# Block sums kept in SBUF for the quarter sums, filter loads moved into the last attention, two convolution steps in halves

## The chip, the cores and the metric

The kernel runs on one core of one Trainium2 chip. The metric is the device time of one execution in microseconds (us). In what follows PE is the matrix engine, DVE the vector engine, ACT the scalar engine, POOL the engine that also issues one set of DMAs, and SP the engine that issues the others. Line numbers (L236) are those of the kernel before.

## The reference, cut to what matters

Two layers run one after the other on x of shape (4, 1024, 32, 32). The first is an attention block with rotary angles and RMS norms over all channels, the second a bottleneck of three convolutions with batch norms.

```python
# layer 0, for 4 batches of N = 1024 tokens, 16 heads of 64
qkv = (x @ w_qkv.T + b_qkv).reshape(B, N, 3, nh, hd)
q, k = rope(q), rope(k)
q = rmsnorm(q.reshape(B, N, inner), q_norm_w);  k = rmsnorm(k.reshape(B, N, inner), k_norm_w)
attn = softmax(einsum('bqhd,bkhd->bhqk', q, k) * hd ** -0.5)
ctx  = einsum('bhqk,bkhd->bqhd', attn, v).reshape(B, N, inner)
x    = rmsnorm(ctx @ w_proj.T, norm_out_w) + x
# layer 1
out = relu(bn(conv1x1(x, w1)));  out = relu(bn(conv3x3(out, w2)));  out = bn(conv1x1(out, w3))
x   = relu(x + softplus(residual_scale)[0] * out)
```

## The kernel before, in words

**Stages.** The batches b = 0 to 3 go one after the other through Q projection, K projection, V projection, attention (two halves c of 512 queries, eight head pairs hp each) and output projection. Then come the first convolution, the 3x3 convolution (written as transforms of input, filter and output around 16 products) and the third convolution. All operands are float32.

**Fast matrix products.** Each projection is a 2x2 block product in seven instead of eight block products. For this the weights need four sums of blocks, S1 to S4, made by four subtractions or additions on DVE. Q and K of batch 0 use one level: `project` (L290 and on) runs, for each of four column groups g, five products of eight matmul records each (S2, S1, S3, S4, A22), after eight products on unsummed blocks. Its sums are made by `operands` (L236 to L239: the third subtraction, L238, makes the operand of the group's first product), from four blocks that SP loads (L226), into a ring of eight chunks `wring`; POOL stores the four sums to DRAM (`wd`, L242). V of batch 0 and everything after it use two levels (`project2`): each of the seven block operands (index k in `OUTER`) is cut into quarters and needs sums of quarters, which lie in DRAM as `wd2`.

**The weight work of batch 0.** What V of batch 0 reads from `wd` and `wd2` is made beside Q and K of batch 0. `prepare_blocks` loads the four blocks of v's weights for one g on POOL's queue (L406), and its `make` forms the four sums on DVE (L409 to L412) and stores them to `wd` (L414). `prepare` does the same one level down: four quarter loads on POOL's queue (L383), four subtractions or additions (L392 to L395), four stores to `wd2` (L397). For k of S1 to S4 the quarters are read back from `wd`. `weight_parts(parts, first, step, lag, alloc)` sets the order: part i is loaded after `first + i * step` products and made `lag` products later. In Q of batch 0 the parts are the four blocks of v and v's quarters k = 0, 1, 6, 2, in the tile `unused`; in K of batch 0 v's quarters 3, 4, 5 and then q's quarters k = 0 for the next batches, in the tile `room` (traced as `rq`), which V writes afterwards.

**Order.** PE and POOL, and in the main region DVE and ACT too, execute in the order in which the program emits the steps: `after(n, step)` emits a step n products later, `waiting` holds the steps of the rotary turn (`turn(f)`, L701 for q: two products with sin and cos on DVE and two accumulating DMAs on POOL, L705) that fill DVE's spare time. `turn` writes into one of three `big_temp` buffers, so it waits until the DMAs of the turn three before have read theirs. SP's order is left to a scheduler. POOL's DMAs take eight completion semaphores in turn, so that each waits for the one eight before it.

**Filters.** `filters()` loads nine pieces of the 3x3 filter on SP (L1053) into the tiles T0 to T2 (traced as `t_w`), and returns five steps that transform them; the attention of the last batch spreads the steps over its head pairs as `extra`. In SP's built order the nine loads stand among those of v's weights of the last batch, three at a time.

**Rotary tables.** The tables cos and sin are multiplied by the row norm in place (L693) and so are loaded again on POOL's queue after every use (L176, L177).

**Convolutions.** `across(i, j)` and `down(b, i, row, j)` are the two steps of the input transform, both through `differences` (L1325); `first_channels` runs them for batch 0 and the first 128 channels, between the last matmuls of the first convolution. After the 3x3 convolution, when the statistics are complete, the norm and Relu of h2 run tile by tile, batches 0 and 2 on ACT (L1428) and 1 and 3 on DVE (L1430, L1431), ahead of the third convolution (L1526), whose first group takes the batches in order.

Of the kernel before, what the change touches and what calls it, by code (L numbers as in the profile page):

```python
# [12 lines left out]
AF = mybir.ActivationFunctionType  # L13
ALU = mybir.AluOpType
# [7 lines left out]
NT = C // P  # L22
# [7 lines left out]
NPT = PL // P  # L30
# [4 lines left out]
WQ, WK, WV, WP, W1 = 0, NFB, 2 * NFB, 3 * NFB, 4 * NFB  # L35
# [27 lines left out]
NG = NT // 2  # L63
QH = P // 4
SUMS = ("S2", "S1", "S3", "S4")
OUTER = ("A11", "A12", "S2", "S3", "S1", "S4", "A22")
TARGET = ("22", "11", "12", "21", "22", "12", "21")
QT = CH // 2
# [17 lines left out]
def program(ctx, tc, x, wblk, w2, w3, vecs, cos, sin, out, bad):  # L86


    nc = tc.nc
# [62 lines left out]
    wd2 = dram.tile([4, len(OUTER), len(SUMS), P, CH], F32, name=f"wd2{u}")  # L152
# [5 lines left out]
    with tc.tile_pool(name=f"st{u}", bufs=2) as st, ExitStack() as s:  # L158
# [26 lines left out]
        half = [slice(c * CH, (c + 1) * CH) for c in range(NCH)]  # L185
# [68 lines left out]
        def after(n, step):  # L254
            later.append((pace["at"] + n, step))
# [145 lines left out]
        def prepare_blocks(base, g, alloc, queue):  # L401

            a11, a12, a21, a22 = a = alloc(f"blk_{base}_{g}")
            for i, t in enumerate(a):
                ih = i % 2
                queue.dma_start(t, wblk[base + g + NG * (i // 2)][:, ih * NH * P : (ih + 1) * NH * P])  # L406

            def make():
                nc.vector.tensor_tensor(a22, a21, a22, ALU.add)  # L409
                nc.vector.tensor_tensor(a21, a11, a21, ALU.subtract)  # L410
                nc.vector.tensor_tensor(a11, a22, a11, ALU.subtract)
                nc.vector.tensor_tensor(a12, a12, a11, ALU.subtract)  # L412
                for o, t in enumerate((a11, a22, a21, a12)):
                    nc.gpsimd.dma_start(wd[base // NT * NG + g, o], t)  # L414

            return make

# [628 lines left out]
        def filters():  # L1046

            steps = []
            raw = t_tiles("w2")
            taps = w2.rearrange("p (c k f) -> p c k f", c=NPT, k=9)  # L1050
            for dy in range(3):
                for dx, slot in enumerate((0, 1, 3)):
                    nc.sync.dma_start(  # L1053
                        raw[dy][:, slot, :].rearrange("p (c f) -> p c f", c=NPT), taps[:, :, 3 * dy + dx, :]
                    )
            two = [tp.tile([P, 2, CH], F32, tag=n, name=f"u2_{n}") for n in ("cos", "sin")]

            def sums_of(g0, g1, g2, new):

                nc.vector.tensor_tensor(new, g0, g2, ALU.add)  # L1060
                nc.scalar.mul(g1, g1, 0.5)
                nc.vector.scalar_tensor_tensor(g1, new, 0.5, g1, ALU.mult, ALU.add)
                nc.vector.tensor_tensor(new, new, g1, ALU.subtract)

            for dy in range(3):
                r = raw[dy]
                steps.append(lambda r=r: sums_of(r[:, 0], r[:, 1], r[:, 3], r[:, 2]))
            for h in range(2):
                js = slice(2 * h, 2 * h + 2)
                steps.append(lambda h=h, js=js: sums_of(*(raw[dy][:, js] for dy in range(3)), two[h]))  # L1070
            for i in range(4):
                for j in range(4):
                    uw[i, j] = two[j // 2][:, j % 2] if i == 2 else raw[(0, 1, None, 2)[i]][:, j]
            return steps
# [19 lines left out]
        def weight_parts(parts, first, step, lag, alloc):  # L1094

            for i, part in enumerate(parts):
                after(first + i * step, lambda part=part: after(lag, part(alloc, nc.gpsimd)))

        def pieces_of(tile, cols=NCH):

            at = deque(tile[:, i, h] for i in range(tile.shape[1]) for h in half[:cols])

            def alloc(name):
                at.rotate(-4)
                return [at[i] for i in range(-4, 0)]

            return alloc


        parts_of = {  # L1110
            base: [
                lambda alloc, queue, which=which, base=base, k=k: prepare(which, base, k, alloc, queue)
                for k in range(len(OUTER))
            ]
            for which, base in enumerate((WQ, WV, WP, WK))
        }

        def blocks_of(base):
            return [lambda alloc, queue, g=g: prepare_blocks(base, g, alloc, queue) for g in range(NG)]
# [15 lines left out]
        room = v_room("rq_0")  # L1135
        for b in range(B):
# [7 lines left out]
            two = (0, *two2[0], False) if b > 0 else None  # L1144
            if b == 0:
                unused = kp.tile([P, NT, N], F32, tag="k", name="unused")
                parts = blocks_of(WV) + [parts_of[WV][k] for k in (0, 1, 6, 2)]
                weight_parts(parts, 8, 2.4, 4, pieces_of(unused))
            elif b == 1:
                weight_parts([parts_of[WK][5]], 9, 0, 4, pieces_of(room[:, : NT // 2, :]))  # L1150
            tq = qk_proj(b, WQ, xs[b], ts[b], "bq", q_all, "q", w1 if b == 0 else None, two, True)
# [3 lines left out]
                ahead.append(two2[2][:2])  # L1155
            two = (3, *two2[1], False) if b > 0 else None
            if b == 0:
                parts = [parts_of[WV][k] for k in (3, 4, 5)] + [parts_of[WQ][0]]
                weight_parts(parts, 2, 4.5, 4, pieces_of(room))
            tk = qk_proj(b, WK, xs[b], ts[b], "bk", k_all, "k", None, two)  # L1160
            rope(b, k_all, tk, eps_rms, 1.0 / C, (wqk_other, wqk), "k")
            v = room
# [56 lines left out]
            if b + 1 < B:  # L1219
# [3 lines left out]
                for j in range(NT):  # L1223

                    def load(b=b, i=rows[j]):
                        for c in range(NCH):
                            load_x(b + 1, c, (i,))
# [99 lines left out]
        def across(i, j):  # L1327

            d = pad[i].rearrange("p r (c q) -> p q r c", q=2)
            differences(cols[:, j], (d[:, 0, :, :TC], d[:, 1, :, :TC], d[:, 0, :, 1:], d[:, 1, :, 1:]), j)  # L1330

        def down(b, i, row, j=None):

            if (b, i) not in vt:
                vt[b, i] = vp.tile([P, 4, 4, TR * TC], F32, tag=f"V{b % 2}{i}", name=f"V_{b}_{i}")
            if j is None:
                d = cols.rearrange("p j (r q) c -> p q j r c", q=2)
                e = d[:, 0, :, :TR], d[:, 1, :, :TR], d[:, 0, :, 1:], d[:, 1, :, 1:]
                out = vt[b, i][:, row].rearrange("p j (r c) -> p j r c", r=TR)
            else:  # L1340
                d = cols[:, j].rearrange("p (r q) c -> p q r c", q=2)
                e = d[:, 0, :TR], d[:, 1, :TR], d[:, 0, 1:], d[:, 1, 1:]
                out = vt[b, i][:, row, j].rearrange("p (r c) -> p r c", r=TR)
            differences(out, e, row)

        def transform(b, i):
            return [lambda j=j: across(i, j) for j in range(4)] + [lambda r=r: down(b, i, r) for r in range(4)]
# [4 lines left out]
        def first_channels():  # L1352
            norm1(0)
            fill(0, 0)
            for step in transform(0, 0):
                step()
            fill(1, 0)

        def other_channels():
# [44 lines left out]
        def outputs(b, f, h):  # L1404

            ox, oy, m1, m2 = banks[b, f, h]
            n = nq[h] = acc.tile([P, 2, CH], F32, tag="tot", name=f"n_{b}_{f}_{h}")
            nc.vector.tensor_tensor(n[:, 0], ox, m2, ALU.add)
            nc.vector.tensor_tensor(n[:, 1], m1, oy, ALU.subtract)
            if h == 0:  # L1410
                return
            i0, i1, i2, i3 = (nq[i // 2].rearrange("p q (i t) -> p i q t", i=2)[:, i % 2] for i in range(4))
            y = h2[b, f] = h2_all[:, b * NPT + f, :]
            yv = y.rearrange("p (r s c q) -> p s q r c", r=TR, s=2, c=TC)
            vs = big_temp(f"y_{b}_{f}")
            for s_, (op, i, op1) in enumerate(((ALU.add, i0, ALU.add), (ALU.subtract, i3, ALU.subtract))):
                v = vs[:, half[s_]].rearrange("p (q t) -> p q t", q=2)
                nc.vector.scalar_tensor_tensor(v, i1, col("b2", f), i2, ALU.add, op)
                v, i = (a.rearrange("p q (r c) -> p q r c", r=TR) for a in (v, i))
                nc.vector.tensor_tensor(yv[:, s_], v, i, op1)  # L1420
            for c in range(NCH):
                nc.vector.bn_stats(h2stats[:, f, b * NCH + c, :], y[:, half[c]])
            if b == B - 1:
                n2 = norm_of(h2stats[:, f], col("g2", f), col("be2", f), f"2_{f}")
                for i in range(B):
                    z = h2[i, f]
                    if i % 2 == 0:
                        nc.scalar.activation(z, z, AF.Relu, bias=n2[1], scale=n2[0])  # L1428
                    else:
                        nc.vector.tensor_scalar(z, z, n2[0], n2[1], ALU.mult, ALU.add)  # L1430
                        nc.vector.tensor_scalar(z, z, 0.0, None, ALU.max)  # L1431

        h2_all = kp.tile([P, NT, N], F32, tag="k", name="h2")
        w3t = [[chunk(f"w3_{k}_{g}") for g in range(NT // NH)] for k in range(NPT)]
# [187 lines left out]
```

## Time and profile before

| | us |
|---|---|
| median of 3 runs | 2679.48 (2679.37 to 2683.2) |
| the profiled execution, its own time | 2678.03 |
| span of the profiled execution | 2676.1 |
| PE busy within the span | 2646.2 |
| DVE, ACT, POOL busy | 2108.7, 1111.9, 464.7 |

Busy times count the instructions that compute and the issue of POOL's DMAs. A wait is idle time of an engine, put down to what ended it. Start times are counted from the start of the span. The profiled execution takes 1.9 us more than its span.

### The profile page before, as it was taken

The page shows a single profiled execution, that of the slowest core. Times are in us where ns is not written, and L with a number is a line of the kernel's source. Part 1 is how long each engine was busy: PE and PEld are TensorE (multiplying, and loading weights), DVE is VectorE, ACT ScalarE, POOL GpSimd, SP SyncE. Part 2 cuts the span into 40 slices and gives each one's busy share as a digit, 9 for nine tenths or more (in the row PEclk, how much of TensorE's full clock was granted, in tenths as well). Part 3 has the DMA queues.
Part 4 walks back from the last instruction along what each step waited for, and adds up shares of the span by engine and source line. Part 5 has one row for each costly group of instructions (what it writes and reads, how often), then busy time and mean ns, then how long its engine had stood idle before and what let it go on. Part 6 is the DMA issues. An engine that isn't in the chain of part 4 may idle for free. (4 is left out here: it accounts for less than half of the span.)

```text
span 2676.1 us, 32605 instructions
## 1 busy us (share of the span) xinstructions
PE 2646.2 (99%) x11354; PEld 1652.0 (62%) x11354; DVE 2108.7 (79%) x2528; ACT 1111.9 (42%) x1547; POOL 464.7 (17%) x568
## 2 busy tenths in 40 slices
PE   9999999999999999999999999999999999999997
PEld 4448533488888333688886333888884335846843
DVE  5577899998787866888879667887978678877987
ACT  2222455523442655433343555233525654312266
POOL 2551233301001221200111222100111211010000
PEclk9999999999999999999999999999999999999999
DMA  7897766667567451446675541665783313583165
GB/s 277 315 288 205 209 230 220 231 210 242 174 183 217 80 104 44 157 151 224 190 197 146 92 77 32 214 207 173 193 233 87 69 40 114 172 281 100 63 237 204
DMA packets 258252, 460.28 MB, mean 172 GB/s; under 512 B 35552, under 2 KB 130576, under 8 KB 258080
## 3 DMA queue, kind: packets, MB, share of 16 engines
q1 hardware_dynamic: 213552, 309.09, 35.6%
q0 software_dynamic: 44528, 149.02, 21.8%
q8 instruction: 93, 1.52, 0.2%
q14 instruction: 79, 0.65, 0.1%
HBM read 331.62 MB, written 97.01 MB: 160 GB/s over the span
## 5 line engine op out<-in xcount | busy, mean ns | idle before, releaser
L772 ACT ACTIVATE p<-sc 128x1024 f32<-128x1024 f32 x512 | 476.2, 1045 | 26.2 <-PE sc L765 24.7
L765 PE MATMUL sc<-q,k 64*128 64x512 f32 x2048 | 457.5, 596 | 0.0
L778 DVE TENSOR_TENSOR den<-den,p 128x1024 f32<-128x1024 f32 x336 | 413.5, 1231 | 36.1 <-DVE den L778 0.9
L765 PEld LDWEIGHTS sc<-q,k 64*128 64x128 f32 x2048 | 190.3, 186 | 264.8 <-issue 121.7
L786 PE MATMUL cx<-p,to 128*64 128x512 f32 x1536 | 340.2, 595 | 0.0
L786 PEld LDWEIGHTS cx<-p,to 128*64 128x64 f32 x1536 | 106.0, 137 | 228.6 <-issue 228.6
L458 PE MATMUL p_v<-w_v,x 128*128 128x256 f32 x928 | 210.0, 379 | 1.4 <-DVE x L429 1.4
L463 PE MATMUL p_y<-q,w_y 128*128 128x256 f32 x928 | 209.8, 379 | 0.0
L743 POOL TENSOR_SCALAR q<-q,vec 128x512 f32<-128x512 f32 x64 | 128.3, 2012 | 452.5 <-DVE q L742 444.5
L463 PEld LDWEIGHTS p_y<-q,w_y 128*128 128x128 f32 x928 | 176.0, 190 | 27.1 <-issue 3.4
L458 PEld LDWEIGHTS p_v<-w_v,x 128*128 128x128 f32 x928 | 176.1, 190 | 26.7 <-DVE x L429 2.4
L791 ACT COPY q<-cx 128x512 f32<-128x512 f32 x64 | 37.5, 586 | 359.1 <-PE cx L786 359.1
L776 DVE TENSOR_TENSOR den<-p 128x1024 f32<-128x1024 f32 x56 | 69.2, 1235 | 132.3 <-ACT p L772 132.3
L463 PE MATMUL p_q<-to,w_q 128*128 128x256 f32 x672 | 152.2, 379 | 0.0
L463 PE MATMUL p_k<-to,w_k 128*128 128x256 f32 x672 | 152.2, 379 | 0.0
L463 PEld LDWEIGHTS p_k<-to,w_k 128*128 128x128 f32 x672 | 127.4, 190 | 18.4 <-issue 1.2
L463 PEld LDWEIGHTS p_q<-to,w_q 128*128 128x128 f32 x672 | 127.4, 190 | 18.4 <-issue 1.2
L786 PE MATMUL cx<-p,rq 128*64 128x512 f32 x512 | 113.4, 595 | 0.0
L1526 PE MATMUL c<-h,w 128*128 128x512 f32 x256 | 110.3, 592 | 0.9 <-ACT h L1428 0.9
L705 POOL DMA_DIRECT2D k<-ks x64 | 57.0, 1066 | 220.5 <-ACT p L772 78.0
L458 PE MATMUL p_v<-w_v,t 128*128 128x256 f32 x384 | 90.1, 379 | 0.8 <-DMA w_v<-wdf 0.8
L463 PE MATMUL p_y<-to,w_y 128*128 128x256 f32 x384 | 90.1, 379 | 0.0
(486 smaller groups left out, 4220.3 us busy)
## 6 DMA issues: line engine op xcount, KB each, us to landing
w_v<-wd2f SPq DMA_DIRECT2D x112, 256.0 KB
w_y<-wd2f SPq DMA_DIRECT2D x112, 256.0 KB
w_q<-wd2f SPq DMA_DIRECT2D x84, 256.0 KB
w_k<-wd2f SPq DMA_DIRECT2D x84, 256.0 KB
wd2f<-w_pre POOLq DMA_DIRECT2D x68, 256.0 KB, 3.9
x<-in_x_dram SPq DMA_DIRECT2D x64, 256.0 KB
q<-qs POOLq DMA_DIRECT2D x64, 256.0 KB, 5.5
k<-ks POOLq DMA_DIRECT2D x64, 256.0 KB, 4.4
```

The lines of the kernel that those rows point to most:

```text
L458: nc.tensor.matmul(o[:, q].rearrange("p (g f) -> p g f", g=2), r[:, i, q * P : (q + 1) * P], wt[:, :, i, :], skip_group_check=True, **at,)
L463: nc.tensor.matmul(o[:, q], wt[:, q, i, :], r[:, i, :], skip_group_check=True, **at)
L705: nc.gpsimd.dma_start(dst[i::2, f, :], other[1 - i :: 2, :], accum_op=ALU.add)
L743: nc.gpsimd.tensor_scalar(cx, cx, col("bv", hp), None, ALU.add)
L765: nc.tensor.matmul(sc[:, j], k_all[d, hp, t * P : (t + 1) * P], q_all[d, hp, at], start=True, stop=bad is not None,)
L772: nc.scalar.activation(p, sc, AF.Exp)
L776: nc.vector.tensor_tensor(d_, probs[0], p, ALU.add)
L778: nc.vector.tensor_tensor(d_, d_, p, ALU.add)
L786: nc.tensor.matmul(o[j * HD : (j + 1) * HD, :], v[:, t, h0 : h0 + HD], probs[t][:, j], start=(t == 0), stop=(t == N // P - 1),)
L791: nc.scalar.copy(q_all[:, hp, at], o)
L1526: nc.tensor.matmul(os[i], w3t[k][f // NH][:, f % NH, :], h2[b, k][:, half[c]], start=(k == 0), stop=(k == NPT - 1),)
```

## The change

There are four edits.

1. The sums of v's blocks are made in the tile `room` (new `stay`): block sum o of group g stays at `room[:, 2 * o + g // 2, half[g % 2]]`. v's quarter sums for k = 2 to 5 are no longer prepared from quarters read back from DRAM, but in place from these (new `prepare_there`), after 1, 4, 7 and 10 products of K; their stores to `wd2` take pieces of 256 elements instead of 512 out of SBUF. v's quarters 0, 1 and 6 stay as they were. q's part 0 is loaded after 14 products of K and made 4 later.
2. `filters` loads its nine pieces on POOL's queue, and the loads become the first of now six `extra` steps of the last attention.
3. `first_channels` transforms the columns j = 1, 2 first (two `across`, four `down`), then 0 and 3.
4. The norm of h2 splits every batch's tile: the first 512 positions on ACT, the second 512 on DVE.

```diff
+        def stay(tile, g):
+            return lambda name: [tile[:, 2 * o + g // 2, half[g % 2]] for o in (0, 3, 2, 1)]
+
+        def prepare_there(which, k, tile):
+            o = SUMS.index(OUTER[k])
+            a11, a12, a21, a22 = (
+                tile[:, 2 * o + oq, :].rearrange("p (g f) -> p g f", g=2)[:, :, iq * QT : (iq + 1) * QT]
+                for oq in range(2) for iq in range(2)
+            )
+            def make():
+                nc.vector.tensor_tensor(a22, a21, a22, ALU.add)
+                nc.vector.tensor_tensor(a21, a11, a21, ALU.subtract)
+                nc.vector.tensor_tensor(a11, a22, a11, ALU.subtract)
+                nc.vector.tensor_tensor(a12, a12, a11, ALU.subtract)
+                for m, t in enumerate((a11, a22, a21, a12)):
+                    nc.gpsimd.dma_start(wd2[which, k, m].rearrange("p (g f) -> p g f", g=2), t)
+            return make
...
-            for dy in range(3):
-                for dx, slot in enumerate((0, 1, 3)):
-                    nc.sync.dma_start(
-                        raw[dy][:, slot, :].rearrange("p (c f) -> p c f", c=NPT), taps[:, :, 3 * dy + dx, :]
-                    )
+            def load():
+                for dy in range(3):
+                    for dx, slot in enumerate((0, 1, 3)):
+                        nc.gpsimd.dma_start(
+                            raw[dy][:, slot, :].rearrange("p (c f) -> p c f", c=NPT), taps[:, :, 3 * dy + dx, :]
+                        )
+            steps.append(load)
...
-                parts = blocks_of(WV) + [parts_of[WV][k] for k in (0, 1, 6, 2)]
-                weight_parts(parts, 8, 2.4, 4, pieces_of(unused))
+                parts = [
+                    lambda alloc, queue, g=g: prepare_blocks(WV, g, stay(room, g), queue) for g in range(NG)
+                ]
+                weight_parts(parts + [parts_of[WV][k] for k in (0, 1, 6)], 8, 2.4, 4, pieces_of(unused))
...
-                parts = [parts_of[WV][k] for k in (3, 4, 5)] + [parts_of[WQ][0]]
-                weight_parts(parts, 2, 4.5, 4, pieces_of(room))
+                for i, k in enumerate((2, 3, 4, 5)):
+                    after(1 + 3 * i, prepare_there(1, k, room))
+                weight_parts([parts_of[WQ][0]], 14, 0, 4, pieces_of(room[:, : NT // 2, :]))
...
-            if j is None:
-                d = cols.rearrange("p j (r q) c -> p q j r c", q=2)
+            if j is None or isinstance(j, slice):
+                js = slice(0, 4) if j is None else j
+                d = cols[:, js].rearrange("p j (r q) c -> p q j r c", q=2)
...
-            for step in transform(0, 0):
-                step()
+            for js in (slice(1, 3), slice(0, 4, 3)):
+                for j in range(4)[js]:
+                    across(0, j)
+                for row in range(4):
+                    down(0, 0, row, js)
             fill(1, 0)
...
-                    z = h2[i, f]
-                    if i % 2 == 0:
-                        nc.scalar.activation(z, z, AF.Relu, bias=n2[1], scale=n2[0])
-                    else:
-                        nc.vector.tensor_scalar(z, z, n2[0], n2[1], ALU.mult, ALU.add)
-                        nc.vector.tensor_scalar(z, z, 0.0, None, ALU.max)
+                    z, z1 = (h2[i, f][:, h_] for h_ in half)
+                    nc.scalar.activation(z, z, AF.Relu, bias=n2[1], scale=n2[0])
+                    nc.vector.tensor_scalar(z1, z1, n2[0], n2[1], ALU.mult, ALU.add)
+                    nc.vector.tensor_scalar(z1, z1, 0.0, None, ALU.max)
```

In the built program PE's instructions keep their order. On DVE in K of batch 0, the quarter sums k = 2 and 3 now both stand ahead of the reciprocal of q's norm, k = 4 behind the sums of K's group 0, k = 5 between q's turns 0 and 1 and so ahead of the sums of K's group 1; none stands between the sums of groups 1 and 2; q's part 0 and then turn 7 stand between those of groups 2 and 3. On POOL the four loads of q's part 0 stand between turns 3 and 4, ahead of the stores of K's group 2, where they stood behind them.

More of the change, by code (lines that the diff above doesn't have):

```diff
@@ L1335, in down @@
                 vt[b, i] = vp.tile([P, 4, 4, TR * TC], F32, tag=f"V{b % 2}{i}", name=f"V_{b}_{i}")
-            if j is None:
-                d = cols.rearrange("p j (r q) c -> p q j r c", q=2)
+            if j is None or isinstance(j, slice):
+                js = slice(0, 4) if j is None else j
+                d = cols[:, js].rearrange("p j (r q) c -> p q j r c", q=2)
                 e = d[:, 0, :, :TR], d[:, 1, :, :TR], d[:, 0, :, 1:], d[:, 1, :, 1:]
-                out = vt[b, i][:, row].rearrange("p j (r c) -> p j r c", r=TR)
+                out = vt[b, i][:, row, js].rearrange("p j (r c) -> p j r c", r=TR)
             else:
```

## The prediction

> **What bounds the kernel now.** I read the page's busy shares first, then the list of PE's waits, then the order of time of PE, DVE and POOL around each wait.
>
> ```profile
> span 2676.1 us, 32605 instructions
> PE 2646.2 (99%) x11354; PEld 1652.0 (62%) x11354; DVE 2108.7 (79%) x2528; ACT 1111.9 (42%) x1547; POOL 464.7 (17%) x568
> ```
>
> PE works 2646.2 of 2676.1 us and no edit changes its instructions, so at most some 30 us are to be had; about 6 of these lie before the first x arrives and some 15 after the last matmul (it starts at 2659.8), where nothing is edited. What remains is in PE's waits:
>
> ```profile
> PE pa_k L303 <- DVE w_k_3b L238: 2.3, 1, 2.3
> PE c2x L1385 <- DVE V L1325: 1.5, 2, 1.0
> PE p_v L458 <- DVE x L429: 1.4, 2, 1.2
> PE c L1526 <- ACT h L1428: 0.9, 1, 0.9
> PE p_v L458 <- DMA w_v<-wdf: 0.8, 1, 0.8
> ```
>
> The longest is in K of batch 0. First PE, then DVE, then POOL around it, in order of time (start, duration, instruction, in brackets the idle time before it and its releaser):
>
> ```profile
> 180.59 3.60 PE L303 MATMUL pa_k<-t,w_k_2b 128*128 128x512 f32 x8
> 186.52 5.40 PE L303 MATMUL pa_k<-t,w_k_3b 128*128 128x512 f32 x8 [2.34 <-DVE w_k_3b L238]
> 191.76 3.60 PE L303 MATMUL pc_k<-t,w_k_3b_s 128*128 128x512 f32 x8
> ```
>
> ```profile
> 181.54 0.69 DVE L392 TENSOR_TENSOR rq<-rq 128x512 f32<-128x512 f32 x1 [6.07 <-DMA rq<-in_wblk_dram]
> ...
> 185.78 0.69 DVE L238 TENSOR_TENSOR w_k_3b<-w_k_3b_s,w_k_3b 128x512 f32<-128x512 f32 x1
> ```
>
> ```profile
> 167.09 0.59 POOL L242 DMA_DIRECT2D wdf<-w_k_2b  x1 [0.42 <-DVE w_k_2b L238]
> ...
> 174.68 0.72 POOL L383 DMA_DIRECT2D rq<-in_wblk_dram  x1 [1.10 <-DMA q<-qs]
> ```
>
> DVE stood 6.07 us in front of q's part 0, whose last load POOL issued at 174.68, because POOL had first to wait for group 2's sums (L242, 167.09). Group 3's sums, four instructions behind on DVE, came at 186.47. Undisturbed products start 3.43 us apart (170.29, 173.72, 177.15, 180.59), so the next but one was due at 187.45 and came at 191.76: 4.31 us lost, the wait and the slow matmuls after it. Group 2 lost 0.41 us before (166.75 against 149.28 + 17.16 = 166.44, its second product 170.29 against 169.88).
>
> **The second place** is V of batch 3, beside the same spot of batch 2:
>
> ```profile
> 1409.08 5.45 PE L458 MATMUL p_v<-w_v,x 128*128 128x256 f32 x24 [0.24 <-DVE x L429]
> 1982.91 5.45 PE L458 MATMUL p_v<-w_v,x 128*128 128x256 f32 x24 [1.20 <-DVE x L429]
> ```
>
> ```profile
> 1980.30 1.23 DVE L693 TENSOR_TENSOR cosT<-cosT,sqk 128x1024 f32<-128x1024 f32 x1 [0.50 <-DMA cosT<-in_cos_dram]
> ```
>
> ```profile
> 1968.34 1.29 SPq L1053 DMA_DIRECT2D t_w<-in_w_dram  x2
> ```
>
> DVE's sums for PE stand behind the multiplication of the reloaded tables. The tables' loads are issued 11.6 us before PE needs the sums in both batches, but cos lands after 8.3 us in batch 2 and after 9.3 us in batch 3, where three filter pieces (0.75 MB) went out at the same moment.
>
> [...] here 2.34 us of idle were followed by eight matmuls in 5.40 instead of 3.60 us[...]. [...] the new stores have runs of 1 KB. Of such runs the trace has only loads (rq<-wdf, 6.0 us to landing).
>
> **Edit 1, part by part.** *Removed:* 16 quarter loads (4 MB) on POOL at 0.72 us of issue (L383), 11.5 us. *Changed:* 16 stores, 0.54 us each (L397); in 1 KB runs I take 0.72 us, the price of L383, so +2.9 us. POOL issues 8.6 us less in Q and K. DVE's instructions stay as many: 16 of 0.69 us. *Moved*, with DVE's queue recounted from the durations above:
> - k = 2 and 3 (5.7 us) fall into DVE's idle time ahead of the reciprocal at 120.22 (9.88 us idle before it). Cover: that gap.
> - k = 4 follows group 0's sums, k = 5 follows turn 0. Group 1's sums, at 141.25 before, now wait for 2.9 us more behind k = 5 and 0.7 us of k = 4: I get L236 at 145.0 and L238 done at 147.1; PE wants it at 149.28. So 2.2 us of slack, down from 5.9. This wait is new; behind it stand turns 2 to 5.
> - Between groups 1 and 2 two preparations (5.7 us) are gone. Turns 2 to 5 run from 149.1, turn 5 after turn 2's DMAs (issued 151.6 to 153.3, landing 7 us later, at 160.3): group 2's L238 is done at 162.8 to 164.9, PE wants it at 166.45. The 0.41 us go.
> - POOL comes to q's part 0 after turn 3, at 156.2 instead of 170.77, because group 2's stores are now behind it. Its loads land at 159.1 + 6.7 = 166; DVE, after group 2's sums and turn 6, comes at 168.6. No wait; done at 171.4. Turn 7 and two additions end at 175.2.
> - Group 3's sums then need their fourth block. SP loads it into a chunk that PE frees at 169.9 and a store of group 2 frees. That store goes out behind turn 5, at 163.1 instead of 167.09, and lands after 6.9 us at 170.0; the block lands 6.4 us later, at 176.5; L238 is done at 178.6. PE wants it at 183.6. Late next is this block, with 5 us of slack. The 4.31 us go.
>
> In Q the block sums only change their tile; parts 0, 1, 6 keep their places. K's rotary loads and group 3's stores move ahead with DVE, SP's loads of v's weights wait for them less. Gain: **4.72 us**.
>
> **Edit 2.** The three pieces leave the moment of the cos load. Batch 2 shows the place without them: 0.24 instead of 1.20 us of wait, so **0.96 us** (bounds: 0, if the difference was chance, and 1.20). POOL issues nine loads, about 1 us each with semaphore waits, near 2060, ahead of turn 7's DMAs (2076), a batch of bias additions (L743, 2 us each) and the residual DMAs. Turn 7 is wanted by head pair 7 at 2117: some 30 us of cover. SP loses them. The filter steps move by up to two head pairs; PE ran without a wait through all of this attention, DVE has 4.4 us idle in half of its head pairs.
>
> **Edit 3.** DVE pays four instructions more: two half-size `down` (128x256 costs 0.38, 128x1024 1.22, so 0.65) for each whole one: 8 x 0.65 against 4.63 us, +0.6 us, ending at about 2433.6. It then waits anyway for ACT's last h at 2435.77. PE took its first V at 2434.88 without a wait, so nothing is gained. ACT's `fill(1, 0)` is released 2.6 us later (2430.9) and holds back one h, which then ends at 2432.9; the last one starts at 2435.08, so 2.2 us of cover. **0.** The 1.5 us wait for V follow from that last h and stay.
>
> **Edit 4.** PE's third convolution waited for ACT's first whole tile:
>
> ```profile
> 2555.83 2.38 ACT L1428 ACTIVATE h<-h,sh,sc 128x1024 f32<-128x1024 f32 x2 [0.81 <-DVE sh L1037]
> 2557.13 8.42 PE L1526 MATMUL c<-h,w 128*128 128x512 f32 x19 [0.93 <-ACT h L1428]
> ```
>
> One tile takes 1.24 us, half a tile 0.69 (ACT L1533, 128x512): **0.55 us** earlier. The second half is wanted 0.86 us later; DVE gives it after about 0.45 + 0.40 us (halves of 0.81 and 0.69, rounded up), just in time. ACT then has 4 x 0.69 against 2.38 us before its next evictions[...].
>
> **Sum.** 4.72 + 0.96 + 0.55 = 6.2 us against the profiled execution's 2678.03: 2671.8. The median shown is 1.45 us above that execution; against it, 2679.48 - 6.2 = 2673.2 us. 0.2% is 5.4 us, about what a measurement of this kernel can tell from no change; the working lands 0.9 us beyond it.
>
> **Rivals.** *The hole in K moves instead of closing.* For it: only 2.2 us of slack at group 1 and 1.5 at group 2, and DMA landings between 90 and 200 us vary from 5 to 10 us at a bus busy up to 100%. A lag of 1 to 3 us there costs itself and up to 1.8 us of slow clock; with edits 2 and 4 a net gain of 1.5 to 4 us stays: 2675.5 to 2678. Against it: 4 MB less of traffic. *Edit 1 does not shorten the wait at all* because part 0's loads again land late: only 0.96 + 0.55 remain, 2678. I put these two together. *Slower:* the 1 KB stores of k = 5 land late and hold POOL's eight semaphores. Group 1's third store waits for k = 5's first (issued at 141.9), turn 2's DMAs for its third (143.3); with a landing time L, turn 5 starts at about 151 + L and group 2's sums end at 155.6 + L. PE idles from L = 10.9 us on, microsecond for microsecond, and 1.8 us more for the clock. It takes L of about 21 us to eat the 6.2 us and 5.4 more: 2685 and above. Stores to wd2 from rq landed after 7.9 us, the slowest load after 10.6, which speaks against it.
>
> **How the numbers follow.** Working as written, 0.68, at 2672 to 2674.7; the hole moves or stays, 0.24, at 2675 to 2679; slower, 0.08. The wait on w_v<-wdf (0.8 us) is a matter of DMA timing and may come or go, within these bounds. Of the first case some four fifths lie beyond 5.4 us: faster 0.54; same 0.38; slower 0.08. The range runs from 2671.3 (all, and that wait gone) to 2679, which leaves out the slower case and the outer parts of the others.
>
> **What would show it.** Right: PE's list has no wait on w_k_3b L238; K's products are 3.43 us apart throughout; DVE has no idle time before q's part 0; cos in batch 3 lands in about 8.3 us and p_v waits about 0.2 us; c L1526 waits under 0.4 us; the span is 6 us shorter. Wrong: a wait on w_k_1b or w_k_2b L238, POOL's stores from rq landing after more than 11 us, or a new wait of PE in the last attention.

## The result, and the profile after

The changed kernel takes 2675.41 us (median of 20 executions, 2672.46 to 2678.45), the kernel before 2679.43 us (20 executions, 2676.13 to 2684.05). The ratio is 0.9985 with a 95% interval of 0.9978 to 0.9991, so it is faster by 4.0 us, between 2.4 and 5.9. The profiled executions are 5.57 us apart (2672.46 and 2678.03), but that of the changed kernel is the fastest of its 20.

Line numbers are now those of the kernel after: L303 keeps its number, V's L458 is L480, the third convolution's L1526 is L1559. First the busy shares of the page and then PE's list of waits (what was waited for, us in total, times, longest):

```profile
PE 2645.2 (99%) x11354; PEld 1651.0 (62%) x11354; DVE 2109.3 (79%) x2540; ACT 1112.8 (42%) x1551; POOL 461.8 (17%) x561
```

```profile
PE pa_q L303 <- DMA x<-in_x_dram: 6.0, 1, 6.0
PE c2x L1420 <- DVE V L1355: 1.5, 2, 1.0
PE p_y L485 <- DVE rec L889: 0.9, 1, 0.9
PE p_v L480 <- DVE x L451: 0.7, 2, 0.4
PE c L1559 <- ACT h L1462: 0.5, 1, 0.5
...
PE p_v L480 <- DMA w_v<-wdf: 0.3, 1, 0.3
```

The wait on w_k_3b L238, 2.3 us before, is gone. PE, DVE and POOL in K of batch 0, in order of time:

```profile
180.20 3.60 PE L303 MATMUL pa_k<-t,w_k_2b 128*128 128x512 f32 x8
183.63 3.67 PE L303 MATMUL pa_k<-t,w_k_3b 128*128 128x512 f32 x8
187.14 3.60 PE L303 MATMUL pc_k<-t,w_k_3b_s 128*128 128x512 f32 x8
```

```profile
181.41 0.69 DVE L236 TENSOR_TENSOR w_k_3b_s<-w_k_3b,w_k_3b 128x512 f32<-128x512 f32 x1 [5.71 <-DMA wd2f<-rq]
...
182.86 0.69 DVE L238 TENSOR_TENSOR w_k_3b<-w_k_3b_s,w_k_3b 128x512 f32<-128x512 f32 x1
```

```profile
155.80 3.58 POOL L383 DMA_DIRECT2D rq<-in_wblk_dram  x4
...
165.96 0.59 POOL L242 DMA_DIRECT2D wdf<-w_k_2b  x1 [1.10 <-DVE k L321]
```

PE's products start 3.43 us apart up to 183.63, and 3.51 once. DVE no longer waits in front of q's part 0. It waits 5.71 us one step later, in front of group 3's first sum. That sum needs the fourth block, the block needs the chunk that group 2's first store frees, and POOL issued this store at 165.96. It landed at 175.11, and SP issued the block's load at 175.25. (The bracket names a store of q's part 0 that landed at the moment at which DVE went on. In e2 it names the block's load, and in e4, where the block is loaded early, DVE does not wait.) L238 ends at 183.55, 0.1 us before PE takes it.

V of batch 3 and the third convolution, each with its releaser's engine:

```profile
1978.23 5.45 PE L480 MATMUL p_v<-w_v,x 128*128 128x256 f32 x24 [0.23 <-DVE x L451]
```

```profile
1975.62 1.22 DVE L715 TENSOR_TENSOR cosT<-cosT,sqk 128x1024 f32<-128x1024 f32 x1 [0.44 <-DMA cosT<-in_cos_dram]
```

```profile
2552.28 7.99 PE L1559 MATMUL c<-h,w 128*128 128x512 f32 x18 [0.50 <-ACT h L1462]
```

```profile
2551.42 2.93 ACT L1462 ACTIVATE h<-h,sh,sc 128x512 f32<-128x512 f32 x4 [0.81 <-DVE sh L1059]
```

The waits here fell from 1.20 to 0.23 us and from 0.93 to 0.50 us.

### The profile page after: what moved, and what is told of

Read it like the earlier page. It is cut to its first block, busy times and chain, and to the rows that moved or that the text cites. A ratio compares the mean times of both kernels' runs of the same rounds, so it can differ in the third digit from the quotient of the medians.

```text
span 2670.6 us, 32584 instructions
## 1 busy us (share of the span) xinstructions
PE 2645.2 (99%) x11354; PEld 1651.0 (62%) x11354; DVE 2109.3 (79%) x2540; ACT 1112.8 (42%) x1551; POOL 461.8 (17%) x561
## 3 DMA queue, kind: packets, MB, share of 16 engines
q8 instruction: 93, 1.52, 0.2%
## 5 line engine op out<-in xcount | busy, mean ns | idle before, releaser
L787 PEld LDWEIGHTS sc<-q,k 64*128 64x128 f32 x2048 | 189.8, 186 | 265.5 <-issue 121.3
L480 PE MATMUL p_v<-w_v,x 128*128 128x256 f32 x928 | 210.1, 379 | 0.7 <-DVE x L451 0.7
L480 PEld LDWEIGHTS p_v<-w_v,x 128*128 128x128 f32 x928 | 176.1, 190 | 26.0 <-DVE x L451 1.7
L1559 PE MATMUL c<-h,w 128*128 128x512 f32 x256 | 110.3, 592 | 0.5 <-ACT h L1462 0.5
L480 PE MATMUL p_v<-w_v,t 128*128 128x256 f32 x384 | 90.1, 379 | 0.3 <-DMA w_v<-wdf 0.3
```

Source lines behind the costliest of these rows:

```text
L480: nc.tensor.matmul(o[:, q].rearrange("p (g f) -> p g f", g=2), r[:, i, q * P : (q + 1) * P], wt[:, :, i, :], skip_group_check=True, **at,)
L787: nc.tensor.matmul(sc[:, j], k_all[d, hp, t * P : (t + 1) * P], q_all[d, hp, at], start=True, stop=bad is not None,)
L1559: nc.tensor.matmul(os[i], w3t[k][f // NH][:, f % NH, :], h2[b, k][:, half[c]], start=(k == 0), stop=(k == NPT - 1),)
```

## The experiments

To compare K between runs I use one number, called **K's loss**: from the start of group 1's last product to the start of V, less the 37.77 us that this takes where no product is held up (run e4: 163.38 to 201.15). It is 205.49 - 163.02 - 37.77 = 4.70 us in the first profiled execution of the kernel before and 200.88 - 163.03 - 37.77 = 0.08 us in that of the changed one. It does not count what happens ahead of group 1's last product. Times are medians, set against executions of the kernel before on the same chip; K's loss comes from one profiled execution of each run.

**e1: the changed kernel again**, no edit.

> The changed kernel unaltered, a second profiled execution of it. The profile after has no wait in K of batch 0, but group 3's sums were ready only 0.1 us before PE wanted them (L238 done at 183.55, product due at 183.63). Theory A (the reserve in K is used up, so that a slightly later transfer reopens the hole): in this execution the fourth block of group 3 can be late; a wait of PE on w_k_3b L238 of 0 to 2 us plus slow matmuls, and a median some 3 us above the 2672.5 of the first profiled execution, about 2675.4. Theory B (the spread of the times has nothing to do with K): products of K again 3.43 us apart, no wait on w_k_3b, and the 3 us between executions lie in waits elsewhere (w_v<-wdf, rec, cosT), if this execution is slower at all. Median the same, 2675.4.

Measured: 2675.46 us against 2680.26 (0.9984, 0.9977 to 0.9991). The profiled execution took 2674.49 us. K's loss was 0.13 us. PE's waits in it:

```profile
PE p_q L485 <- DMA w_q<-wdf: 1.6, 1, 1.6
PE c2x L1420 <- DVE V L1355: 1.5, 2, 1.0
PE p_v L480 <- DMA w_v<-wdf: 1.3, 1, 1.3
PE p_y L485 <- DMA w_y<-wdf: 0.5, 1, 0.5
```

It speaks for theory B. The span is 2.1 us longer than in the first execution of the changed kernel, and the three waits on weights are 1.1, 1.0 and 0.5 us longer, other waits slightly shorter. K has no part in it.

**e2: edit 1 alone.** Edits 2, 3 and 4 are replaced by the code before.

```diff
-                        nc.gpsimd.dma_start(
+                        nc.sync.dma_start(
...
-            steps.append(load)
...
-            for js in (slice(1, 3), slice(0, 4, 3)):
+            for step in transform(0, 0):
...
-                    z, z1 = (h2[i, f][:, h_] for h_ in half)
+                    z = h2[i, f]
```

> Edit 1 alone; the filter loads, the first transform and the last norm are as before. By the steps of the prediction: 4.72 us under the kernel before, no wait on w_k_2b or w_k_3b, waits of 1.2 us on x in V of batch 3 and of 0.9 us on h as before; about 2674.7 against 2679.4. Theory A: the median falls by less, 2.5 to 3.5 us, because K's hole reopens in part in many executions. Theory B: the median falls by the whole 4 to 4.7 us.

Measured: 2677.47 us, 2.8 us under 2680.26 (0.9989, 0.9981 to 0.9998). K's loss is 0.24 us. V of batch 3 waits 0.93 us for x, the third convolution 0.93 us for h. The gain is of the size that theory A gave, but its reason is not seen: K lost next to nothing in this execution too. This is the fastest of the 13, though, so it does not show what K loses in the slower ones.

**e3: edits 2, 3 and 4 without edit 1.** The two places of Q and K that edit 1 touches are as before.

```diff
...
-                for i, k in enumerate((2, 3, 4, 5)):
-                    after(1 + 3 * i, prepare_there(1, k, room))
-                weight_parts([parts_of[WQ][0]], 14, 0, 4, pieces_of(room[:, : NT // 2, :]))
+                parts = [parts_of[WV][k] for k in (3, 4, 5)] + [parts_of[WQ][0]]
+                weight_parts(parts, 2, 4.5, 4, pieces_of(room))
```

> Edits 2, 3 and 4 without edit 1: v's quarters 2 to 5 are again read back from DRAM. By the steps of the prediction: 0.96 + 0 + 0.55 = 1.5 us under the kernel before (after the sizes seen in the trace, 0.97 + 0.43 = 1.4), about 2678.0; the wait of about 2.3 us on w_k_3b and the slow matmuls after it as before. Theory A: the same, and edit 1's share of the median gain of 4 us is the remaining 2.6. Theory B: these three bring nothing that shows in the median, or lose something, 2679.4 or more, and edit 1 brings all.

Measured: 2678.16 us, 2.1 us under 2680.26 (0.9993, 0.9985 to 1.0002). The parts add up: 2.8 + 2.1 = 4.9, and all four edits together brought 4.8 in the same comparison. In K the hole is back, but K's loss is 2.08 us and not 4.70. PE waited 1.52 us, and the matmuls after the wait took 3.70 us, not 5.40. This raised the question of what the hole usually costs.

**e5 and e6: the kernel before, two further executions**, no edit.

> The kernel before unaltered, a second profiled execution. In its first one, K of batch 0 lost 4.31 us at group 3: 2.34 us of wait and then eight matmuls in 5.40 instead of 3.60 us. With edit 1 undone in the changed kernel (run e3) the same place lost 1.52 us of wait and no slow matmuls. Theory C (the loss in K is usually the smaller one, so the prediction took an untypical execution for the price of the hole): the wait is 1.4 to 1.8 us, the matmuls after it take 3.6 to 3.7 us, and V of batch 0 starts about 203.5 instead of 205.5. Theory D (the small loss in e3 was itself the exception): 4.3 us lost again, V starts at 205.5. On the V of batch 3: a wait on x of 0.9 to 1.2 us if the filter loads cause it, 0 to 0.5 if the first execution was chance.

> The kernel before unaltered, a third profiled execution; the same expectations as for the second. With one more, K's loss at group 3 is known from three executions (and from e3 a fourth with the same K): theory C expects the slow matmuls in a minority of them, theory D in all but e3.

Measured: 2676.59 and 2676.92 us, each one execution, against a median of 2679.76 for this kernel on the same chip. PE in K of e5, in order of time:

```profile
181.35 3.60 PE L303 MATMUL pa_k<-t,w_k_2b 128*128 128x512 f32 x8
186.44 3.70 PE L303 MATMUL pa_k<-t,w_k_3b 128*128 128x512 f32 x8 [1.49 <-DVE w_k_3b L238]
189.97 3.60 PE L303 MATMUL pc_k<-t,w_k_3b_s 128*128 128x512 f32 x8
```

And the same product in e6:

```profile
186.86 3.70 PE L303 MATMUL pa_k<-t,w_k_3b 128*128 128x512 f32 x8 [1.42 <-DVE w_k_3b L238]
```

K's loss is 2.30 and 2.25 us. With e3 these are three executions of the old K near 2.2 us and one of 4.70, as theory C expected. But four executions, of which e5 and e6 are some 3 us faster than the median, do not show which kind is the usual one.

K's loss also makes the hole look cheaper than it was. PE's first eight matmuls, after the wait for the first x, took 4.93 us or more in every profile, where eight undisturbed ones take 3.43 to the start of the next, and in e3, e5 and e6 they took longest. From 7 to 14 us, in the first execution of the kernel before and in e5 (columns: length, busy time of PE, PEld, DVE, ACT, POOL with counts, granted clock, DMA share, GB/s):

```profile
7.00:14.00 7.00, 7.00 (x15) 3.10 (x14) 1.14 (x8) 1.86 (x3) 0.00 (x0) 1.00 1.04 374
7.00:14.00 7.00, 7.00 (x13) 2.88 (x12) 1.14 (x8) 1.30 (x3) 0.00 (x0) 1.00 1.03 376
```

The first eight matmuls took 5.15 us in the first execution and 6.28 to 6.43 us in e3, e5 and e6. In these three PE so came to K later and waited less for sums that were as late: group 3's first product started 180.5 us after the first matmul in the first execution and 180.7 to 181.0 us in the three. From the first matmul to V it was 199.5 us in the first and 198.0 to 198.3 in the three, against 194.8 to 195.4 in the five executions with edit 1 whose K lost at most 0.24 us (the changed kernel's first, e1, e2, e4, e8; mean 195.1). Counted so, the old order cost 4.4 us in the first execution and about 3.1 in the three.

V of batch 3 waited 1.03 and 1.11 us for x.

**e4: the changed kernel with a reserve for group 3.** Its fourth block and its first sum lie in a free row of room. The block is loaded early on POOL's queue.

```diff
+            if spare and g == NG - 1:
+                a21 = block(base, g + NG, 0, f"{name}_20")
+                a22, s1 = (t.rearrange("p (a b) -> p a b", a=NH) for t in spare)
...
+            spare[:] = [room[:, 5, h] for h in half] if b == 0 else []
+            if spare:
+                last = wblk[WK + 2 * NG - 1][:, NH * P :]
+                after(7, lambda: nc.gpsimd.dma_start(spare[0], last))
...
```

> The changed kernel, but the fourth block and the first sum of K's group 3 in batch 0 lie in a free row of the tile room instead of the ring of eight chunks; the block is loaded on POOL's queue after 7 products of K, so it waits for no store of group 2. Nothing else moves. Group 3's sums should start right behind turn 7 and be ready at about 178 instead of 183.6. Theory A: with 5 us of reserve K's hole stays shut in every execution; median 2 to 3 us under that of the changed kernel, 2672.5 to 2673.5, and less spread. Theory B: the reserve is of no use, the median is that of the changed kernel within 0.7 us. A worse outcome is open: the added load on POOL at 134 us can hold up the turns by about 0.6 us.

Measured: 2675.09 us, against 2680.26 before and 2675.46 for the changed kernel beside it (to before: 0.9982, 0.9973 to 0.9990). The sum that PE waits for, on DVE (L242 here is L238 of the changed kernel):

```profile
177.19 0.69 DVE L242 TENSOR_TENSOR w_k_3b<-rq,w_k_3b 128x512 f32<-128x512 f32 x1
```

It ends at 177.88 and PE takes it at 183.98: 6.1 us of reserve instead of 0.1, and 0.4 us of time, which is less than these runs can tell from nothing. The 2 to 3 us of theory A are not there.

**e7: the kernel before with q's part 0 loaded early.** The order alone is changed, the read-back stays.

```diff
-                parts = [parts_of[WV][k] for k in (3, 4, 5)] + [parts_of[WQ][0]]
-                weight_parts(parts, 2, 4.5, 4, pieces_of(room))
+                parts = [parts_of[WV][k] for k in (3, 4, 5)]
+                pieces_ = pieces_of(room)
+                weight_parts(parts, 2, 4.5, 4, pieces_)
+                weight_parts([parts_of[WQ][0]], 14, 0, 4, pieces_)
```

> The kernel before, with one number changed: q's part 0 is loaded after 14 products of K instead of 15.5, so that POOL issues its four loads ahead of turn 4 and of group 2's stores. The 4 MB of read-back, and the two preparations between groups 1 and 2, stay. Theory order: it is the place of these four loads that makes the hole; they land 10 us earlier, DVE does not wait in front of q's part 0, group 3's sums are ready in time, and K loses nothing at group 3; the time falls by what first alone brought, about 2.8 us, or somewhat less since group 2's 0.2 to 0.4 us stay. Theory traffic: POOL and the DMA engines are still too busy with the read-back; DVE still waits for the loads or for the fourth block, a wait of PE on w_k_3b of over 1 us stays, and the time falls by under 1 us.

Measured: 2681.61 us, 1.9 us above 2679.76 (1.0007, 0.9998 to 1.0015). DVE and POOL:

```profile
185.19 0.69 DVE L236 TENSOR_TENSOR w_k_3b_s<-w_k_3b,w_k_3b 128x512 f32<-128x512 f32 x1 [6.22 <-DMA wd2f<-rq]
```

```profile
171.23 0.60 POOL L242 DMA_DIRECT2D wdf<-w_k_2b  x1 [0.51 <-issue]
```

DVE indeed does not wait in front of q's part 0 (it makes it at 172.32). But the four loads push group 2's stores on POOL from 167.09 to 171.23, the load of group 3's fourth block goes out at 178.42 instead of 174.99, and PE waits 2.48 us. K's loss is 5.01 us. In this execution the early place by itself only changed which transfer was late.

**e8: the changed kernel with q's part 0 loaded late.**

```diff
-                weight_parts([parts_of[WQ][0]], 14, 0, 4, pieces_of(room[:, : NT // 2, :]))
+                weight_parts([parts_of[WQ][0]], 15.5, 0, 4, pieces_of(room[:, : NT // 2, :]))
```

> The changed kernel, with one number changed: q's part 0 is loaded after 15.5 products of K, as in the kernel before, so that its loads stand behind turn 5 and group 2's stores on POOL and its sums behind turn 7 on DVE. The read-back stays away. Theory order: the hole comes back, a wait of PE on w_k_3b of 1 us or more, time 1.5 to 3 us above the changed kernel. Theory traffic: without the read-back the loads go out near 169 instead of 171 to 175 and land by 177; DVE makes the sums by 183; PE loses under 0.5 us, and the time is that of the changed kernel.

Measured: 2675.56 us, 4.2 us under 2679.76 (0.9981, 0.9974 to 0.9987), the same gain as the changed kernel's. DVE in K:

```profile
178.50 0.69 DVE L392 TENSOR_TENSOR rq<-rq 128x512 f32<-128x512 f32 x1 [5.08 <-DMA rq<-in_wblk_dram]
...
182.73 0.69 DVE L238 TENSOR_TENSOR w_k_3b<-w_k_3b_s,w_k_3b 128x512 f32<-128x512 f32 x1
```

DVE waits in front of q's part 0 as in the kernel before, but only until 178.50 instead of 181.54, and PE loses nothing (K's loss 0.0 us). So theory order falls: the hole is closed by the rest of edit 1 (the read-back gone, the sums made earlier), and not by where q's part 0 stands.

**e9: e8 with the loads of the read-back put back**, unread.

```diff
+                def load_again(k):
+                    for i in range(4):
+                        quarter(k_all[:, NT - 2 + i // 2, half[i % 2]], WV, k, i // 2, i % 2, nc.gpsimd)
+                for n, k in ((2, 3), (6.5, 4), (11, 5)):
+                    after(n, lambda k=k: load_again(k))
```

> The kernel of run e8 (the changed kernel, q's part 0 loaded after 15.5 products), with 12 quarter loads of 256 KB added on POOL's queue at the times at which the kernel before reads back k = 3, 4 and 5 (after 2, 6.5 and 11 products). They fill a part of k that is not yet in use and nobody reads them. Theory POOL (the read-back made the hole by its issue time, 12 x 0.72 = 8.6 us, and its 3 MB of traffic): POOL comes to q's part 0 later than 167.15, near 170, the hole of 1 us or more on w_k_3b is back and the time rises by 1.5 to 3 us. Theory place (the hole came from the preparations of k = 4 and 5 and their stores standing between groups 1 and 2): POOL has had these loads ahead of turn 2 and catches up; L238 of group 2 stays at 164 to 165, no hole, the time of e8 within 0.8 us.

Measured: 2676.80 us, 3.1 us under 2679.93 (0.9989, 0.9982 to 0.9995). DVE at turn 5, and PE at group 2's first product:

```profile
164.11 1.22 DVE L723 TENSOR_TENSOR qs<-q,sinT 128x1024 f32<-128x1024 f32 x1 [6.10 <-DMA q<-qs]
```

```profile
168.70 3.70 PE L303 MATMUL pa_k<-t,w_k_2b 128*128 128x512 f32 x8 [1.23 <-DVE w_k_2b L238]
```

A hole comes back, but at group 2 and not at group 3 as in the kernel before, so neither theory had it right. The last four loads go out ahead of turn 2 and delay its DMAs from 151.92 to 154.89. Turn 5 needs turn 2's buffer and waits 6.10 instead of 2.74 us, and group 2's sums stand behind it. K's loss is 1.53 us.

**e10: e8 with the four preparations at the old places**, without read-back.

```diff
-                for i, k in enumerate((2, 3, 4, 5)):
-                    after(1 + 3 * i, prepare_there(1, k, room))
+                for n, k in ((1, 2), (6, 3), (10.5, 4), (15, 5)):
+                    after(n, prepare_there(1, k, room))
```

> The kernel of run e8, with the four preparations in place moved back to where the kernel before makes them (after 1, 6, 10.5 and 15 products); no read-back. On DVE the order in K is then that of the kernel before. Theory place: DVE comes to turn 5 at 162.9 and group 2's L238 ends at 167.4 again, 0.3 us late; its stores go out at 167, q's part 0 behind them; a wait of 1.4 us or more on w_k_3b; time 2 us above e8, about that of the kernel with edits 2 to 4 alone. Theory POOL: group 2 may lose 0.3 us, but without the read-back q's part 0 lands in time and group 3 waits under 0.5 us.

Measured: 2677.90 us, 2.0 us under 2679.93 (0.9992, 0.9983 to 1.0000). Group 3's first product on PE:

```profile
183.97 3.70 PE L303 MATMUL pa_k<-t,w_k_3b 128*128 128x512 f32 x8 [0.29 <-DVE w_k_3b L238]
```

Group 2 loses nothing, group 3 waits 0.29 us, K's loss is 0.55 us: in K it went as theory POOL had it. On DVE the order in K is that of the kernel before, and what is gone from POOL's queue there are the loads of the read-back. Turn 2's DMAs on POOL, in the kernel before and in e10:

```profile
153.69 1.74 POOL L705 DMA_DIRECT2D q<-qs  x2 [0.74 <-ACT k L311]
151.01 1.91 POOL L727 DMA_DIRECT2D q<-qs  x2
```

The rest follows from this: turn 5 starts at 159.55 instead of 162.16, group 2's first store goes out at 164.39 instead of 167.09, and the last load of q's part 0 at 171.24 instead of 174.68. PE's first matmul started at the same time in both, 6.02 and 6.03.

So the profiles of e9 and e10 both say that the loads of the read-back weigh more in K than the place of the sums. The medians do not: e10 gains 2.0 us and e9 3.1 (their intervals overlap), where e8 gains 4.2, and 2.0 is about what edits 2 to 4 brought alone (e3), as theory place had it. The profiled execution of e10 has other waits (2.36 us for x in V of batch 1, 1.3 us on w_v), but whether these belong to the edit is open.

**e11 and e12: the length of the hole set by hand.** DVE's first sum of group 3 is done four and seven times.

```diff
+            for _ in range(3 if name == "k_0_3b" else 0):
+                nc.vector.tensor_tensor(s1, a21, a22, ALU.add)
             nc.vector.tensor_tensor(s1, a21, a22, ALU.add)
```

> The changed kernel with DVE's first sum of K's group 3 in batch 0 done four times instead of once: 3 x 0.72 us later. It sets the length of PE's wait there to about 2.1 us, between the waits of 1.42 to 1.52 us after which eight matmuls took 3.70 us and those of 2.34 and 2.48 after which they took 5.40. Theory step (a wait beyond some length costs a fixed 1.8 us of slow matmuls): 3.70 or 5.40, nothing between. Theory slope (the slow part grows with the wait): about 4.9.

> The same with that sum done seven times: 6 x 0.72 us later, a wait of about 4.3 us. Theory step: the eight matmuls after it take 5.40 us again. Theory slope: 7 us or more.

Measured: 2678.00 and 2682.73 us. Group 3's first product, in e11 and in e12 (lines are two further down):

```profile
185.91 5.40 PE L305 MATMUL pa_k<-t,w_k_3b 128*128 128x512 f32 x8 [2.55 <-DVE w_k_3b L240]
```

```profile
187.95 6.50 PE L305 MATMUL pa_k<-t,w_k_3b 128*128 128x512 f32 x8 [4.30 <-DVE w_k_3b L240]
```

And e12 by stretches of 2 us (length, busy time of PE, PEld, DVE, ACT, POOL with counts, granted clock, DMA share, GB/s):

```profile
187.00:189.00 2.00, 1.05 (x2) 0.53 (x3) 1.93 (x4) 0.00 (x0) 0.81 (x2) 0.50 0.61 240
...
193.00:195.00 2.00, 2.00 (x5) 0.91 (x4) 0.00 (x0) 0.52 (x1) 0.00 (x0) 0.85 0.00 0
195.00:197.00 2.00, 2.00 (x6) 0.90 (x5) 0.00 (x0) 0.07 (x1) 0.00 (x0) 1.00 0.56 131
```

After 4.30 us of idle PE's granted clock was 0.50 from 187 to 193 and 0.85 in the 2 us behind, and the eight matmuls took 2.9 us more than 3.60; after 2.34 to 2.55 us they took 1.8 us more; after 1.42 to 1.52 us 0.1. At this place it is neither the pure step nor the slope.

But the length of the wait does not decide alone. In e10 PE waited 2.36 us in V of batch 1:

```profile
836.54 5.45 PE L480 MATMUL p_v<-w_v,x 128*128 128x256 f32 x24 [2.36 <-DVE x L451]
```

These 24 matmuls took 5.45 us, no more than after the wait of 0.23 us in V of batch 3 (above). And after the wait for the first x, 5.45 to 6.04 us in all fourteen profiles, the first eight matmuls took anything from 4.93 to 6.43 us, 1.5 to 3.0 more than undisturbed ones. What else decides was not tested.

No version tried beats the changed kernel by more than can be told: e4 and e8 lie within 0.4 us of it.

## Why the prediction was right or wrong

**The direction and the range were right, the amount was 2.2 us too large.** Forecast were 6.2 us, measured 4.0 (2.4 to 5.9), and the case that had the most weight, a gain of more than 5.4 us, did not come. 2675.41 us lies within the range given, but in the part that the range owed to its first rival (2675 to 2679) and not in that of the working (2672 to 2674.7).

**Edit 1, the size: this is the step that failed, as far as is known.** The sum took 4.31 + 0.41 us from K of one execution. Of the 4.31, 1.81 us (5.24 us to the next product instead of 3.43) were slow matmuls. In three other executions of the old K the wait was 1.42 to 1.52 us, no slow matmuls followed, and the way to V was about 3.1 us longer than with edit 1 instead of 4.4. With 3.1 for edit 1, 0.9 for edit 2 and 0.4 for edit 4 the sum is 4.4 us, inside the measured interval. But edit 1 alone measured 2.8 us (0.5 to 5.1), which excludes neither price.

**Edit 1, the mechanism: right in the outcome, wrong in what it credited.** K's products run 3.43 us apart and both losses are gone, as written. Group 1's L238 was done at 146.8 (147.1 forecast), group 2's at 164.15 (162.8 to 164.9 forecast), q's part 0 did not wait. But I put the 4.31 us down to POOL coming to q's part 0 at 156.2. Run e8 shows that this place is not needed and e7 that it does not suffice. By the profiles of e9 and e10, one execution each, most of it is the loads of the read-back standing ahead of turn 2 on POOL, and a lesser part the two preparations between groups 1 and 2; the medians do not confirm these shares.

**The 5 us of slack at group 3: wrong, at no cost.** It was 0.1 us. Group 2's first store went out at 165.96 instead of 163.1 and landed after 9.2 instead of 6.9 us, so that DVE could start on the block at 181.41 instead of 176.5. In two further executions with this order (e1, e2) K lost 0.13 and 0.24 us, and 6 us of true reserve in e4 brought nothing that can be told.

**Edit 2: right.** In V of batch 3, five executions with the filter loads on SP waited 0.76 to 1.20 us for x (mean 1.01), nine with the loads in the last attention 0 to 0.51 (mean 0.13): 0.9 us against 0.96. That fits the cause given: cos landed after 8.9 to 9.3 us in the five and after 7.8 to 8.6 in the nine. My comparison with batch 2 was weaker than it looked. There, without any filter load, the wait was anything up to 1.15 us, so 0.96 was in part luck.

**Edit 3: right,** 0. The wait on V is 1.5 us in every profile, with the edit and without.

**Edit 4: mis-sized by 0.12 us.** The wait is 0.92 or 0.93 us in all five executions with whole tiles and 0.49 or 0.50 with halves: 0.43 instead of 0.55. The first half tile took ACT 0.81 us; the 0.69 was the price of another instruction (L1533). The sign "under 0.4 us" was missed.

**The rivals.** The hole that moves or stays had the nearer number (2675.5 to 2678), but not the reason: K lost nothing. The slower case is refuted: the 1 KB stores cost POOL 0.72 us each, as assumed (up to 600 us POOL is busy 189.8 us instead of 198.5, 8.7 less, 8.6 forecast), and landed after 2.5 to 5.6 us, far from the 10.9 from which, by the estimate, they would have delayed PE.

**What stays open.** Executions of one program lie 6 us apart, more than the change brings. e1 shows 2.6 us of it in PE's waits on w_q, w_v and w_y. These sum to 1.3, 1.0 and 0.7 us in three executions of the kernel before and to 0.7 and 3.4 in two of the changed one. Over all fourteen profiles they sum to 0.7 to 1.7 us (mean 1.2) in the four without any of the edits (the kernel before three times, and e7) and to 0.7 to 3.4 (mean 2.4) in the ten with some or all of them. So a part of the gain may be given back there, which would be a second reason for the missing 2.2 us; no run tests it.

## What to carry to other kernels

A hole in the trace has a price per execution (here 4.4 us in one and about 3.1 in three): before a wait is taken as the gain, look whether slow matmuls follow it, get the same place from a second and third execution, and count from a point well ahead of it, since an engine that comes late for another reason waits less (in e3, e5 and e6 the first eight matmuls took 1.1 to 1.3 us longer, and the wait in K was 0.8 to 0.9 us shorter). Taking work off a full queue and moving work within it are two different edits: here moving four loads ahead of their neighbours delayed the next transfers in the chain by 3.4 to 4.1 us (e7), while without the read-back's loads the transfers behind them went out about 3 us earlier (e10). More reserve at a wait that was already closed brought nothing that could be told (e4: 6.1 us of reserve, 0.4 us of time).

## What the runs showed of the hardware

In front of group 3 in K, where eight undisturbed matmuls take 3.60 us, they took 3.70 us after waits of 1.42 (e6), 1.49 (e5) and 1.52 us (e3), 5.40 us after 2.34 (the kernel before), 2.48 (e7) and 2.55 (e11), and 6.50 us after 4.30 (e12). The granted clock was 0.50 in the stretch from 187 to 190 us of the kernel before, from 187 to 189 of e11 and from 187 to 193 of e12, and 1.00 from 186.5 to 190 of the changed kernel, where PE does not wait. So waits of 2.34 to 2.55 us cost 1.8 us more than themselves, and one of 4.30 cost 2.9 more. A wait of 2.36 us in V of batch 1 (e10) cost nothing more: the length alone does not tell, and these runs give no threshold.

In the changed kernel 256 KB stores from SBUF in runs of 1 KB cost POOL 0.72 us of issue each: eight in a row took 5.69 us (at 109.92), four 2.85 us (at 131.35) and four 2.92 (at 144.04). Stores in runs of 2 KB (L242 in the kernel before) cost 0.54 to 0.59. The records of the former are 0.67 to 1.22 us long (median 0.94), but those in a row overlap, so it is the stretch and not the record that gives the price.
